# The discarded output of the norms' square activations: one 2-byte tile becomes two 1-byte tiles used by turns

## The chip, the cores and the metric

The kernel runs on one core of one Trainium2 chip. The metric is device time in microseconds: the median of several executions of the same program. Separately, one execution was recorded by the hardware profiler; everything said of single instructions comes from that one.

## What is computed

The input x has 128 batches of 128 rows by 512 columns (float32), and adj is a sparse 128 by 128 matrix. Two layers follow one another, each with a residual and a layer norm. The reference, cut to what matters:

```python
def _layernorm(x, eps=1e-5):
    m = mean(x, -1); v = var(x, -1)
    return (x - m) / sqrt(v + eps)

# layer 0: A = adj @ x[b]; W1 = W2 = adj, so C - A is the bias alone
out = max(relu(A[:, :, None, :] + (C - A)[:, :, :, None]), -1)   # = relu(rowmax(A) + b)
x = _layernorm(x + out)

# layer 1: 8 heads of 64
q, k, v = split(x @ w_qkv)
attn = softmax(where(adj == 0, -inf, q @ k.T * 64 ** -0.5))
o = (attn @ v) @ w_proj + b_proj
ln = (o - mean(o)) * rsqrt(var(o) + 1e-5) * gamma + beta
x = _layernorm(x + (o + ln))
```

So three variances are needed for each batch: one after layer 0, one inside layer 1 and one at its end.

## The kernel before

A batch is one tile of 128 partitions by 512 float32 columns, and four batches make a group; there are 32 groups. A batch passes through some sixty steps, each a small Python function that records one or a few instructions on one engine. A table of due times (`STEADY` for the groups in the middle, `FIRST` and `LAST` for those at the ends, lines 28 to 327) gives each step of each of the four batches its place relative to its group; `group_plan` collects all steps of all groups, the list is sorted by due time, and the instructions are recorded in that order. Every engine then works through its own queue strictly in this order. Semaphores are put in by the framework from the tiles that the instructions read and write: an instruction that writes a tile waits for those that read or wrote it before, on its own engine too.

Tiles that are reused have their buffer chosen by hand (`HOMES`, from line 342). In PSUM there are four single banks (`ps1`) and two double ones (`ps2`).

The steps that matter here, with their engines:

- TensorE: `dm` and `dd` form the dense products of the query, key and value projections. Each product is formed from three float32r products so that the accuracy of float32 is kept: `product` (lines 805 to 810) adds up eight matmuls in a bank called pm, `product_d` (812 to 815) four in a bank called pd. A name such as pd_(16, 5) means group 16, product 5.
- ScalarE: `main` (line 834) copies a pm bank into its place in qkT or v, which frees that bank; VectorE's `rest` (838) adds the pd bank. `exps` (894) takes the exponentials of the eight heads, each with an accumulated sum. `pln` (909) and `xpl` (708) split float32 tiles into two planes of 16 bits, which a DMA writes out and another reads back transposed. `norm0` (696) and `norm2` (1082) apply a norm.
- ScalarE again: `squares` (1038 to 1042) takes the sum of squares that a variance needs. It has three callers: `sq0` for layer 0 (two of the four batches of a steady group; the other two use VectorE's batch statistics, `bn`), `sq1` for the norm inside layer 1, and `sq2` for the last norm. The activation computes (sum - 512 x)^2, with the row sum as a bias pointer, and its accumulator gives the sum of the squares over a row in float32. This sum is all that is used.
- GpSimd: `sm`, `deviation` (1044 to 1049) and their like turn the sums into means and reciprocal deviations.

The squares themselves have to be written somewhere, though nobody reads them. They go to the tile `square`, 128 by 512 in bfloat16, allocated once at line 542. Each activation is shown in the profile as two rows: ACTIVATE, and ACTIVATION_READ_ACCUMULATOR, which delivers the sum.

In the last group the output projection is formed in plain float32 (`TWO["plain"]`, `po`, line 991) rather than from three products. The change leaves that as it is.

Of the kernel before, what the change touches and what calls it, by code (L numbers as in the profile page):

```python
# [13 lines left out]
AF = mybir.ActivationFunctionType  # L14
# [466 lines left out]
def tile_adj_resnorm_d2(  # L481
# [13 lines left out]
    B, T, D = x.shape  # L495
    P = 128
# [6 lines left out]
    scale = HD ** -0.5  # L503

    const = ctx.enter_context(tc.tile_pool(name="const", bufs=1))
# [33 lines left out]
    bias_sb = const.tile([P, D], FP, name="bias_sb")  # L539
    beta_sb = const.tile([P, D], FP, name="beta_sb")  # L540
    nc.vector.memset(mhalf, -0.5)
    square = const.tile([P, D], mybir.dt.bfloat16, name="square")
    nc.scalar.activation(mhalf, mhalf, AF.Copy)


# [102 lines left out]
    def sq0(b):  # L648
        mv, _, i = of_group(b)
        squares(xs[b], mv[:, i, :])  # L650
# [386 lines left out]

    def squares(src, s):

        nc.scalar.activation(  # L1040
            square, src, AF.Square, bias=s[:, 0:1], scale=-float(D), accum_out=s[:, 1:2],
        )

    def deviation(s, n):
# [6 lines left out]
    def sq1(b):  # L1051
        squares(os[b], s1s[b])
# [16 lines left out]
    def sq2(b):  # L1069
        squares(os[b], s2s[b])  # L1070
# [103 lines left out]
```

## Time and profile before

| | us |
|---|---|
| median of 3 executions | 1839.38 |
| lowest and highest of them | 1838.51 and 1841.58 |
| the profiled execution | 1842.82 |
| its span, first to last instruction | 1841.0 |

In the profiled execution ScalarE ran these groups of instructions among others:

| line | instruction | count | mean ns |
|---|---|---|---|
| 1040 | square of an o tile | 256 | 719 |
| 1040 | square of an xt tile | 62 | 722 |
| 1040 | reading the accumulator (o) | 256 | 190 |
| 644 | layer 0's addition, with a sum, 128 x 512 | 62 | 713 |
| 894 | exponential, 128 x 128 | 1016 | 392 |
| 909 | copy into planes, 128 x 2048 of 16 bits | 124 | 1891 |

How to read the profile: PE is TensorE's matmul row, PEld its weight loads, which run ahead of the matmuls they belong to; ACT is ScalarE, DVE VectorE, POOL GpSimd, SP the queue that issues DMAs. A row of a timeline gives the start, the duration, the engine, the source line, the operation and what it writes and reads; "x4" are four such in a row. Overlapping rows of one engine are two instructions in its pipeline. In a list of waits, "A <- B: total, times, longest" says that A stood idle until B was done. The chain is followed back from the last instruction, at each step to what released it.

### The profile page before, as it was taken

The page shows a single profiled execution, that of the slowest core. Times are in us where ns is not written, and L with a number is a line of the kernel's source. Part 1 is how long each engine was busy: PE and PEld are TensorE (multiplying, and loading weights), DVE is VectorE, ACT ScalarE, POOL GpSimd, SP SyncE. Part 2 cuts the span into 40 slices and gives each one's busy share as a digit, 9 for nine tenths or more (in the row PEclk, how much of TensorE's full clock was granted, in tenths as well). Part 3 has the DMA queues.
Part 4 walks back from the last instruction along what each step waited for, and adds up shares of the span by engine and source line. Part 5 has one row for each costly group of instructions (what it writes and reads, how often), then busy time and mean ns, then how long its engine had stood idle before and what let it go on. Part 6 is the DMA issues. An engine that isn't in the chain of part 4 may idle for free.

```text
span 1841.0 us, 32606 instructions
## 1 busy us (share of the span) xinstructions
PE 1808.0 (98%) x10525; PEld 1422.8 (77%) x10525; DVE 1527.8 (83%) x2539; ACT 1557.0 (85%) x3959; POOL 1287.5 (70%) x1932
## 2 busy tenths in 40 slices
PE   7999999999999999999999999999999999999996
PEld 4877787788777778787877877887877787878874
DVE  6988887888888888878888888888888888888875
ACT  5898888888888888988888988888988888879875
POOL 4265567767767767677676677677677676768878
PEclk9999999999999999999999999999999999999998
DMA  5566656567756576756576656676666776566552
GB/s 148 146 161 184 166 159 162 158 169 197 175 157 164 156 182 182 176 154 166 158 191 173 178 154 160 167 201 172 163 161 152 184 185 173 163 154 175 146 161 69
DMA packets 486714, 303.94 MB, mean 165 GB/s; under 512 B 399504, under 2 KB 403728, under 8 KB 486544
## 3 DMA queue, kind: packets, MB, share of 16 engines
q1 hardware_dynamic: 485680, 300.75, 62.2%
q8 instruction: 83, 1.36, 0.3%
q10 hardware_dynamic: 864, 1.12, 0.2%
q14 instruction: 87, 0.71, 0.1%
HBM read 73.20 MB, written 131.07 MB: 111 GB/s over the span
## 4 chain that ended last, share of the span: by engine, by line
PE 86%; POOL 5%; DVE 4%; ACT 2%; issue 2%; DMA 1%; SPq 0%; POOLq 0%; DVEq 0%; ACTq 0%
PE psc L855 6%; PE pav L941 6%; PE pa L624 5%; POOL sum L1046 1%; DVE o L1034 1%; POOL xb L1027 1%; POOL xb L1031 1%; DVE nmax L877 0%; DVE e L869 0%; POOL xb L1024 0%; DVE o L1061 0%; PE pv L769 0%; POOL sum L1045 0%; ACT e L894 0%; POOL od L741 0%
## 5 line engine op out<-in xcount | busy, mean ns | idle before, releaser
L894 ACT ACTIVATE e<-e,nmax 128x128 f32<-128x128 f32 x1016 | 392.6, 392 | 2.2 <-DVE nmax L877 2.1
L741 POOL TENSOR_TENSOR od<-oh,ol 128x512 fp32r<-128x512 f32 x124 | 164.6, 1328 | 139.4 <-DVE ol L959 77.5
L909 ACT COPY planes<-e 128x2048 uint16<-128x2048 uint16 x124 | 234.4, 1891 | 10.0 <-DVE e L903 5.1
L1046 POOL TENSOR_TENSOR sum<-sum,mhalf 128x1 f32<-128x1 f32 (+1 forms) x287 | 218.2, 760 | 23.9
L1040 ACT ACTIVATE square<-o,sum 128x512 bf16<-128x512 f32 x256 | 184.0, 719 | 22.7 <-DVE o L1034 14.4
L1031 POOL TENSOR_TENSOR xb<-xb,o 128x512 f32<-128x512 f32 x125 | 165.5, 1324 | 52.0 <-DVE o L1034 49.6
L894 ACT ACTIVATION_READ_ACCUMULATOR e<-e,nmax 128x1 f32 x1016 | 194.2, 191 | 0.0
L869 DVE SCALAR_TENSOR_TENSOR e<-psc,mask 128x1024 f32<-128x1024 f32 x127 | 152.5, 1220 | 43.9 <-PE psc L855 41.4
L1027 POOL TENSOR_TENSOR xb<-xb,beta_sb 128x512 f32<-128x512 f32 x128 | 165.7, 1294 | 2.9
L903 DVE TENSOR_TENSOR e<-e,sums 128x1024 f32<-128x1024 f32 x128 | 160.9, 1257 | 1.1
L1061 DVE SCALAR_TENSOR_TENSOR o<-o,sum,gamma_sb 128x512 f32<-128x512 f32 x128 | 103.9, 812 | 69.2 <-POOL sum L1049 65.7
L877 DVE TENSOR_REDUCE nmax<-e 128x8 f32<-128x1024 f32 x127 | 152.9, 1204 | 1.0
L735 POOL TENSOR_SCALAR oh<-oxh 128x512 fp32r<-128x512 f32 x31 | 64.8, 2090 | 116.8 <-DVE oxh L731 33.4
L708 ACT COPY xplanes<-xt 128x1024 uint16<-128x1024 uint16 x124 | 129.2, 1042 | 12.5 <-DMA rowsx<-xplanes 10.3
L624 PE MATMUL pa<-xt,adjT 128*128 128x512 f32 x256 | 133.9, 608 | 1.5 <-DVE rm L635 1.1
L855 PEld LDWEIGHTS psc<-qkT 64*128 64x128 f32 x2048 | 119.6, 188 | 19.8 <-issue 17.5
L855 PE MATMUL psc<-qkT 64*128 64x128 f32 x2048 | 132.4, 279 | 1.0 <-DVE o L1034 0.6
L941 PE MATMUL pav<-eT,v 128*64 128x128 f32 x2048 | 127.0, 276 | 0.9 <-ACT eT L932 0.8
L941 PEld LDWEIGHTS pav<-eT,v 128*64 128x64 f32 x2048 | 110.4, 137 | 17.9 <-issue 8.6
L1024 POOL TENSOR_SCALAR xb<-xb,sum 128x512 f32<-128x512 f32 x128 | 111.1, 868 | 12.2 <-DMA xb<-in_x_dram 12.1
L1034 DVE SCALAR_TENSOR_TENSOR o<-o,sum,xb 128x512 f32<-128x512 f32 x128 | 98.5, 769 | 24.0 <-POOL sum L1046 19.1
L696 ACT ACTIVATE xt<-xt,sum 128x512 f32<-128x512 f32 x128 | 103.3, 809 | 11.9 <-POOL sum L690 11.9
(4263 smaller groups left out, 5512.5 us busy)
## 6 DMA issues: line engine op xcount, KB each, us to landing
rows<-planes SPq DMA_DIRECT2D x124, 512.0 KB, 3.1
xt<-in_x_dram SPq DMA_DIRECT2D x128, 256.0 KB, 3.1
xb<-in_x_dram SPq DMA_DIRECT2D x128, 256.0 KB, 2.9
out_dram<-o SPq DMA_DIRECT2D x128, 256.0 KB, 3.2
rowsx<-xplanes SPq DMA_DIRECT2D x124, 256.0 KB, 2.5
wraw<-in_L_gnn_w_qkv_dram SPq DMA_DIRECT2D x8, 256.0 KB, 3.5
xT<-rowsx SPq DMA_TRANSPOSE x124, 3.8
eT<-rows SPq DMA_TRANSPOSE x124, 5.1
```

The lines of the kernel that those rows point to most:

```text
L624: nc.tensor.matmul(pa[b], adjT, xs[b], start=True, stop=True)
L741: engine.tensor_tensor(d, h.bitcast(FP), l.bitcast(FP), op=ALU.subtract)
L855: nc.tensor.matmul(psc[:, s, hp, :], qkT[hs, hp, i, :], qkT[hs, KC + hp, i, :], start=not with_mask, stop=not with_mask or hp == HP - 1,)
L877: nc.vector.tensor_reduce(nmaxs[b], es[b], AX.X, ALU.max, negate=True)
L894: nc.scalar.activation(es[b][:, j, :], src[:, j, :], AF.Exp, bias=nmax[:, j : j + 1], scale=by, accum_out=sums[b][:, j : j + 1],)
L903: nc.vector.tensor_tensor(es[b], es[b], sums.pop(b)[:, :, None].to_broadcast([P, H, P]), op=ALU.mult,)
L909: nc.scalar.copy(pl, es.pop(b).rearrange("p h m -> p (h m)").bitcast(U16).rearrange("p (m s) -> p s m", s=2),)
L941: nc.tensor.matmul(pavs[b][s * HD : (s + 1) * HD, hp, :], v[:, h * HD : (h + 1) * HD], eT[:, s * HP + hp, :], start=True, stop=True,)
L1027: nc.gpsimd.tensor_tensor(xbs[b], xbs[b], beta_sb, op=ALU.add)
L1031: engine.tensor_tensor(xbs[b], xbs[b], os[b], op=ALU.add)
L1040: nc.scalar.activation(square, src, AF.Square, bias=s[:, 0:1], scale=-float(D), accum_out=s[:, 1:2],)
L1046: nc.gpsimd.tensor_tensor(s, s, mhalf[:, :n], op=ALU.pow)
```

## The change

The tile of 512 bfloat16 values a partition becomes a tile of two halves, each of 512 one-byte unsigned integers a partition. A counter flips at every call of `squares`, and the activation writes to the half that it names. The accumulated sum, its operands and all else stay as they are. The whole of it:

```diff
@@ -539,7 +539,8 @@
     nc.vector.memset(mhalf, -0.5)
-    square = const.tile([P, D], mybir.dt.bfloat16, name="square")
+    junk = const.tile([P, 2, D], mybir.dt.uint8, name="squares")
+    turn = [0]
     nc.scalar.activation(mhalf, mhalf, AF.Copy)
@@ -1037,8 +1038,9 @@
     def squares(src, s):
 
+        turn[0] ^= 1
         nc.scalar.activation(
-            square, src, AF.Square, bias=s[:, 0:1], scale=-float(D), accum_out=s[:, 1:2],
+            junk[:, turn[0], :], src, AF.Square, bias=s[:, 0:1], scale=-float(D), accum_out=s[:, 1:2],
         )
```

## The prediction

> **What bounds the kernel now.** I read the page first (busy shares, then the chain), then the weight-load queue's list of waits, then the timelines of one group, and last each semaphore record of the trace against the wait values in the program.
>
> ```profile
> PE 1808.0 (98%) x10525; PEld 1422.8 (77%) x10525; DVE 1527.8 (83%) x2539; ACT 1557.0 (85%) x3959; POOL 1287.5 (70%) x1932
> ...
> PE 86%; POOL 5%; DVE 4%; ACT 2%; issue 2%; DMA 1%; SPq 0%; POOLq 0%; DVEq 0%; ACTq 0%
> ...
> L1040 ACT ACTIVATE square<-o,sum 128x512 bf16<-128x512 f32 x256 | 184.0, 719 | 22.7 <-DVE o L1034 14.4
> ```
>
> TensorE is busy all the time and carries the chain; ScalarE holds 2% of it. So what the squares cost ScalarE matters only where TensorE waits for ScalarE. The page shows no such wait, since matmul ends are modelled; the weight loads do. In the list of waits of the weight-load queue from 276 to 1600 us, this line stands once for every group from 5 to 28, 24 times, at 0.4 or 0.5 us:
>
> ```profile
> PEld pd_(16, 5)_10122 L815 <- ACT qkT L834: 0.5, 1, 0.5
> PEld pd_(17, 5)_10745 L815 <- ACT qkT L834: 0.5, 1, 0.5
> ```
>
> Group 16 on the PE timeline (start, us, what):
>
> ```profile
> 921.24 0.39 PE L809 MATMUL pm_(16, 6)_10101<-x_h,w_h 128*128 128x512 f32 x1
> 921.47 0.39 PE L810 MATMUL pm_(16, 6)_10101<-x_l,w_l 128*128 128x512 f32 x1
> ...
> 921.92 0.39 PE L810 MATMUL pm_(16, 6)_10101<-x_l,w_l 128*128 128x512 f32 x1
> 922.34 1.19 PE L815 MATMUL pd_(16, 5)_10122<-x_d,w_d 128*128 128x512 f32 x4
> 923.37 0.39 PE L809 MATMUL pm_(16, 5)_10134<-x_h,w_h 128*128 128x512 f32 x1
> ```
>
> Matmuls start 0.227 us apart (921.24 to 921.92 is three steps). From 921.92 to 923.37 are five steps, 1.135 us unhindered; they took 1.45. TensorE loses about 0.31 us here, in each of the 24 groups. It waits for a PSUM bank that ScalarE empties with the copy into qkT. ScalarE ahead of that copy:
>
> ```profile
> 914.29 0.71 ACT L1040 ACTIVATE square<-o,sum 128x512 bf16<-128x512 f32 x1
> 914.90 0.19 ACT L1040 ACTIVATION_READ_ACCUMULATOR square<-o,sum 128x1 f32 x1
> 915.13 0.72 ACT L1040 ACTIVATE square<-o,sum 128x512 bf16<-128x512 f32 x1
> 915.76 0.18 ACT L1040 ACTIVATION_READ_ACCUMULATOR square<-o,sum 128x1 f32 x1
> 915.98 0.72 ACT L1040 ACTIVATE square<-xt,sum 128x512 bf16<-128x512 f32 x1
> 916.61 0.19 ACT L1040 ACTIVATION_READ_ACCUMULATOR square<-xt,sum 128x1 f32 x1
> 916.70 1.89 ACT L909 COPY planes<-e 128x2048 uint16<-128x2048 uint16 x1
> ...
> 921.71 0.57 ACT L834 ACTIVATE qkT<-pm_(16, 8)_10087 128x512 f32<-128x512 f32 x1
> ```
>
> See the seams. 914.90 + 0.19 = 915.09, and the next square starts at 915.13: 0.04 after. At 916.61 + 0.19 = 916.80 the copy had already started (916.70): 0.10 before. A square that follows a square lacks the overlap that every other pair has. From 907.87 (a qkT copy that waits for TensorE) to the end of the copy at 921.71 ScalarE never idles for another engine: this run of work, started by TensorE and awaited by it, is 0.31 us too long.
>
> **What the Trainium skill says.** "ScalarE: Activation LUTs", section What ACT_TABLE_LOAD costs, has one element a cycle for fp32 and bf16 alike, 280 ns + 0.833 ns an element with a pointer bias, and back-to-back activations overlapping by about 93 ns. That gives 706 ns for 512; the squares took 705 to 753, and the seams overlap by 0.09 to 0.10 us: agreed. Of one-byte outputs no page states a rate, and nothing in the trace writes one. "Perfetto Trace Analysis", section DVE / Act Engine Instruction, has the reported end at the acknowledged write, from which the semaphore goes out; so a wait for one's own predecessor costs the whole overlap and a little more, as the 0.04 shows. The same page, Identifying the Most-Contended Engine, calls matmul busy time a poor measure and weight loads a better one: so it is here. Under Identifying Dependency Chains it says that further waits go into a separate instruction ahead; the trace has 78 such on line 1040.
>
> **The change part by part.**
> *Instructions.* Both programs have the same instructions in the same order on every engine, but for 22 more wait-only ones on ScalarE. The tile takes 1024 bytes a partition as before (512 x 2, now 2 x 512 x 1), at the same address. No DMA and no queue moves.
>
> *Removed: the wait for the square just before.* All squares write one tile, so each waits for the last. In 88 places two squares stand side by side; in 84 of them this wait, and nothing else, ended last in the trace (23 or 24 ns before the start); the other four, in the last 13 us, wait for VectorE. With two halves by turns a square waits for the last but one, done long before (the third, at 915.98, would ask for the one that ended at 915.09). Each such place gains 0.04 + 0.09 = 0.13 us.
>
> *Where it counts.* A steady group has three places: 915.13 and 915.98 in the run ahead of TensorE's wait, and 934.10, after which ScalarE waits 0.39 us for a DMA at 936.01 anyway (gain nothing). So the qkT copy comes 0.26 us sooner. Nothing else holds it: in the semaphore records the next-latest release of what lies between came 0.5 us or more before its start (planes 506 ns, o 7.7 us, xt 1.4 us, qkT 1.2 us). 0.26 is less than the 0.31 lost, so all of it reaches TensorE: 24 x 0.26 = 6.2 us.
>
> *What is late next.* The following bank, pm_(16, 5), is freed by the qkT copy at 922.35, which follows TensorE's own pm_(16, 6) and doesn't move: released 0.42 us before its use, about 0.15 us of it spare at the weight load, and a weight load can be 0.1 us late unnoticed (one at 926.06 was 0.17 late and cost 0.06). Enough, or short by 0.02. Other waits later in the group (VectorE's qkT additions) follow TensorE and move with it.
>
> *Two more places.* pd_(2, 9) at 141.18 and pm_(29, 6) at 1650.42 wait for a qkT copy behind one such pair: 0.13 each, 0.26.
>
> *Added.* About 27 xplanes copies get a second wait, for ScalarE itself, long fulfilled. Squares with two waits start 83 ns after VectorE's release, those with one 24, so this may cost 0.06 us each. It falls at 936.01, followed by 0.13 us of idle time at 939.00 and almost 3 us at 952.57: nothing. Without that cover, 1.5 us. Ten squares lose a second wait; at the end four of these lie 0.06 us nearer to VectorE, but GpSimd sets the pace there: nothing.
>
> *One-byte outputs.* From below: no gain, since fp32 and two-byte outputs already run at one rate. From above: if a one-byte write ran at half rate, 512 x 0.833 = 0.43 us a square. I take nothing, by the equal rates of the other types.
>
> *Sum.* 6.2 + 0.26 = 6.5 us. The profiled execution took 1842.82 (span 1841.0), so 1836.3 there; it lay 3.4 above the median. From the median 1839.38: 1832.9.
>
> **The rivals.**
> *A: given back.* Another chain through VectorE or GpSimd is almost as long, and TensorE gets half: 24 x 0.13 = 3.1, 1836.3. For it: the pm_(16, 5) release leaves little, and TensorE waits again at pd_(16, 11). Against: that wait is a round trip with TensorE itself, and the other waits in the group have 0.1 us or more.
> *B: the seam isn't the wait.* If squares miss the overlap for another cause, nothing changes: 1839.4. Against: squares after any copy overlap by 0.10 us, and exponentials with the same bias pointer and accumulator, side by side, overlap too (904.83 + 0.19, next 904.92).
> *C: slower, by the one-byte write.* Between 907.87 and 921.71 stand four squares (908.36 and the three shown). The gain of 0.26 is used up at 0.065 us more a square. Beyond that TensorE waits longer: at 0.21 a square 24 x (0.85 - 0.26) = 14 us, 1854; at the full 0.43, 24 x 1.45 = 35, 1874. For it: this output type is in no row. Against: time follows elements, not bytes, in every row of ScalarE (the uint16 copy of 2048 elements takes 1891 ns, 0.833 each and a constant).
>
> **How the numbers follow.** Likeliest 0.72 (1831 to 1835.5), A 0.14, B 0.05, C 0.09. Forecast 1832.9. A measurement of this kernel can tell about 0.2%, 3.7 us, from no change; the three runs shown spread over 3.1. Faster by more: 0.72 and a fifth of A, 0.75. Within: the rest of A and B, 0.16. Slower: C, 0.09. The range 1830.5 to 1837.0 holds the likeliest case and most of A, and leaves out B, C and the likeliest one's ends. Its upper end takes in the 1.5 us of the uncovered waits.
>
> **What would show it.** Squares at about 720 ns on a uint8 tile; seams between squares at -0.09 in place of +0.04; the 24 lines of pd_(g, 5) in the weight-load waits gone or under 0.2 us; five steps of 1.2 us in place of 1.45 there; groups nearer by 0.26 us. It is wrong if squares last over 780 ns, if the seams stay, or if the lines go and other weight loads wait as long.

## The result, and the profile after

| | before, us | after, us |
|---|---|---|
| median of 5 executions each, same chip | 1839.80 | 1833.06 |
| lowest and highest | 1838.51 and 1841.58 | 1832.4 and 1834.64 |
| the profiled execution | 1842.82 | 1834.2 |
| its span | 1841.0 | 1832.4 |

The ratio is 0.9963, with a 95% interval of 0.9949 to 0.9978: 6.7 us faster. The two profiled executions lie 8.6 us apart. Part of that is not the change: the first qkT copy of all, which runs before the first square, started at 27.77 us instead of 29.47. These 1.7 us are a difference of the two starts.

Three lines of the page after: the busy shares, the chain by engine, and the group of the squares (busy us, mean ns, idle time ahead of them).

```profile
PE 1802.5 (98%) x10525; PEld 1420.9 (78%) x10525; DVE 1526.9 (83%) x2539; ACT 1549.0 (85%) x3959; POOL 1288.8 (70%) x1932
...
PE 86%; POOL 6%; DVE 3%; ACT 2%; issue 1%; DMA 1%; SPq 0%; POOLq 0%; ACTq 0%; DVEq 0%
...
L1042 ACT ACTIVATE squares<-o,sum 128x512 uint8<-128x512 f32 x256 | 183.2, 717 | 21.5 <-DVE o L1035 15.2
```

The page hardly tells the two kernels apart: TensorE bounds both, and one square lasts 717 ns instead of 719. The difference is in how squares follow each other. ScalarE in group 16, from the three squares in a row to the qkT copy that TensorE awaits and the one after it (start, us, what):

```profile
908.37 0.73 ACT L1042 ACTIVATE squares<-o,sum 128x512 uint8<-128x512 f32 x1
908.99 0.20 ACT L1042 ACTIVATION_READ_ACCUMULATOR squares<-o,sum 128x1 f32 x1
909.08 0.73 ACT L1042 ACTIVATE squares<-o,sum 128x512 uint8<-128x512 f32 x1
909.69 0.20 ACT L1042 ACTIVATION_READ_ACCUMULATOR squares<-o,sum 128x1 f32 x1
909.79 0.73 ACT L1042 ACTIVATE squares<-xt,sum 128x512 uint8<-128x512 f32 x1
...
915.52 0.58 ACT L835 ACTIVATE qkT<-pm_(16, 8)_10087 128x512 f32<-128x512 f32 x1
916.43 0.60 ACT L835 ACTIVATE qkT<-pm_(16, 6)_10101 128x512 f32<-128x512 f32 x1 [0.33 <-PE pm_(16, 6)_10101 L811]
```

908.99 + 0.20 is 909.19, and the next square had started at 909.08: it overlaps its predecessor by 0.11 us. At the second seam (909.69 + 0.20, then 909.79) it is 0.10. Before, both seams had a gap of 0.04.

The list of the weight loads' waits from 276 to 1600 us. Of the 24 lines for pd_(g, 5) four are left:

```profile
PEld pd_(5, 5)_3269 L816 <- ACT qkT L835: 0.5, 1, 0.5
PEld pd_(10, 5)_6384 L816 <- ACT qkT L835: 0.4, 1, 0.4
PEld pd_(20, 5)_12614 L816 <- ACT qkT L835: 0.4, 1, 0.4
PEld pd_(15, 5)_9499 L816 <- ACT qkT L835: 0.4, 1, 0.4
```

And TensorE at the same place in group 16:

```profile
916.00 0.39 PE L811 MATMUL pm_(16, 6)_10101<-x_l,w_l 128*128 128x512 f32 x1
916.24 1.11 PE L816 MATMUL pd_(16, 5)_10122<-x_d,w_d 128*128 128x512 f32 x4
917.18 0.40 PE L810 MATMUL pm_(16, 5)_10134<-x_h,w_h 128*128 128x512 f32 x1
```

The five steps from the last matmul of pm_(16, 6) to the first of pm_(16, 5) take 917.18 - 916.00 = 1.18 us, where they took 1.45. Steps of 0.227 would give 1.135. From one pm_(g, 6) to the next an undisturbed group took 55.75 us before and takes 55.49 now: 0.26 less. From the pm_(g, 6) of group 5 to that of group 28, which are 23 such periods, the time went from 1284.11 to 1278.31 us: 5.8 less.

The same place can be read in all 24 groups of both traces. Beyond 1.135 us the five steps cost 7.67 us in sum before. After, they cost 1.93: 0.02 to 0.05 us in each of twenty groups, 0.22 to 0.32 in each of the four with a line above. The one step after them, beyond 0.227 us, cost 0.07 us in sum before and 0.34 after. So TensorE gained 5.5 us here (7.67 + 0.07 - 1.93 - 0.34).

**The four groups that are left.** ScalarE in group 10, with the idle time ahead of an instruction and its releaser in brackets:

```profile
575.84 0.71 ACT L1042 ACTIVATE squares<-xt,sum 128x512 uint8<-128x512 f32 x1
576.45 0.19 ACT L1042 ACTIVATION_READ_ACCUMULATOR squares<-xt,sum 128x1 f32 x1
577.26 1.90 ACT L910 COPY planes<-e 128x2048 uint16<-128x2048 uint16 x1 [0.61 <-DVE e L904]
```

The seam is mended here too, but the copy behind it waits 0.61 us for VectorE, which scales the attention weights at line 904. In groups 5 and 20 the copy waits for the same line, 0.52 and 0.48 us. In group 15 the wait is 0.10 us and too short for a row to name its releaser, but it is VectorE there too:

```profile
853.69 1.31 DVE L904 TENSOR_TENSOR e<-e,sums 128x1024 f32<-128x1024 f32 x1
...
855.03 1.90 ACT L910 COPY planes<-e 128x2048 uint16<-128x2048 uint16 x1
```

853.69 + 1.31 is 855.00, and the copy starts 0.03 us later, as it does in the other three. In group 16 VectorE's release came 506 ns ahead of this copy before the change and 215 ns ahead after it.

The change did not make VectorE late. In the kernel before, the same copy waits for it in groups 5, 15, 20 and 25, by 0.34, 0.34, 0.12 and 0.14 us. Two of these:

```profile
302.43 1.90 ACT L909 COPY planes<-e 128x2048 uint16<-128x2048 uint16 x1 [0.34 <-DVE e L903]
...
860.93 1.90 ACT L909 COPY planes<-e 128x2048 uint16<-128x2048 uint16 x1 [0.34 <-DVE e L903]
```

Where VectorE ends last, a mended seam ahead of it gains nothing. What makes VectorE late was followed in group 10 of the kernel after alone. There VectorE stands idle for 1.05 us up to 570.65, until GpSimd's sums (L1048) are done, and is not idle again before line 904 ends. In group 16 the same idle time is 0.10 us. The sums come behind a small GpSimd instruction (L1051) of 0.67 us that takes 0.22 in group 16. The kernel before has slow small GpSimd instructions in the same groups too (0.65 us in group 10, 0.68 in group 15). What slows them in about every fifth group was not tried.

### The profile page after: what moved, and what is told of

Read it like the earlier page. It is cut to its first block, busy times and chain, and to the rows that moved or that the text cites. A ratio compares the mean times of both kernels' runs of the same rounds, so it can differ in the third digit from the quotient of the medians.

```text
span 1832.4 us, 32628 instructions
## 1 busy us (share of the span) xinstructions
PE 1802.5 (98%) x10525; PEld 1420.9 (78%) x10525; DVE 1526.9 (83%) x2539; ACT 1549.0 (85%) x3959; POOL 1288.8 (70%) x1932
## 4 chain that ended last, share of the span: by engine, by line
PE 86%; POOL 6%; DVE 3%; ACT 2%; issue 1%; DMA 1%; SPq 0%; POOLq 0%; ACTq 0%; DVEq 0%
PE psc L856 7%; PE pav L942 6%; PE pa L625 5%; POOL xb L1028 1%; POOL sum L1048 1%; POOL xb L1032 1%; ACT e L895 1%; DVE o L1035 1%; POOL x_d L742 1%; POOL od L742 1%; POOL xb L1025 1%; POOL sum L1051 0%; DVE o L1063 0%; POOL sum L1047 0%; PE pv L770 0%
## 5 line engine op out<-in xcount | busy, mean ns | idle before, releaser
L1048 POOL TENSOR_TENSOR sum<-sum,mhalf 128x1 f32<-128x1 f32 (+1 forms) x287 | 217.3, 757 | 23.9
L1042 ACT ACTIVATE squares<-o,sum 128x512 uint8<-128x512 f32 x256 | 183.2, 717 | 21.5 <-DVE o L1035 15.2
L1025 POOL TENSOR_SCALAR xb<-xb,sum 128x512 f32<-128x512 f32 x128 | 115.6, 904 | 9.3 <-DMA xb<-in_x_dram 9.2
```

The lines of the kernel that those rows point to most:

```text
L1042: nc.scalar.activation(junk[:, turn[0], :], src, AF.Square, bias=s[:, 0:1], scale=-float(D), accum_out=s[:, 1:2],)
L1048: nc.gpsimd.tensor_tensor(s, s, mhalf[:, :n], op=ALU.pow)
```

## The experiments

My theory: the wait of a square for its predecessor on the one discarded tile kept the two from overlapping; in a steady group only the two seams ahead of the qkT copy of product 8 count, and TensorE gains what that copy gains. The rivals: the shorter output type makes the gain (or costs something); any time taken from ScalarE helps, wherever it lies; or the gain stops at another wait. All runs were timed against the kernel before on the same chip, in five rounds except the last two, in three.

### Is it one byte, or the turns?

`one_byte_one_tile`: the kernel before with the type changed alone.

```diff
-    square = const.tile([P, D], mybir.dt.bfloat16, name="square")
+    square = const.tile([P, D], mybir.dt.uint8, name="square")
```

> One tile of 512 one-byte values for all squares, without turns: each square waits for the one before it again. If the wait between neighbouring squares is what was removed, nothing is gained: 1839.8 us, ratio 1.000, the 24 weight-load waits of pd_(g, 5) back at 0.4 to 0.5 us each. If the one-byte output is what helps (fewer bytes written), all or most of the 6.7 us stay: 1833. If one-byte writes were slower, over 1841.

Measured 1839.21 against 1839.64: 0.9995 [0.9987, 1.0004], no difference. The view by tile of this run (lowest, median and highest ns) and its timeline:

```profile
L1040 ACT ACTIVATE square<-o,sum x256: 706/721/754, 103.9 to 1830.6; 128x512 uint8<-128x512 f32 x128
```

```profile
910.83 0.72 ACT L1040 ACTIVATE square<-o,sum 128x512 uint8<-128x512 f32 x1
911.44 0.20 ACT L1040 ACTIVATION_READ_ACCUMULATOR square<-o,sum 128x1 f32 x1
911.68 0.72 ACT L1040 ACTIVATE square<-o,sum 128x512 uint8<-128x512 f32 x1
```

A one-byte output takes 721 ns, as the two-byte one did. The gap is there: 911.44 + 0.20 = 911.64, next start 911.68. All 24 lines of pd_(g, 5) stay. So the type neither pays nor costs; the gain is that of the turns. The type matters in another way: two halves of one byte fit in the 1024 bytes that one two-byte tile took. Two halves of two bytes don't fit in the memory that is left, so turns with the two-byte type weren't run; that the type has no part in it rests on this run.

### Do only the seams ahead of the awaited copy count?

Two versions of the changed kernel without the counter. The squares all write half 0, but those of the norm inside layer 1 write half 1 for one of the four batches, which mends some seams and leaves others.

```diff
-    turn = [0]
...
-    def squares(src, s):
-
-        turn[0] ^= 1
+    def squares(src, s, half=0):
+
...
-            junk[:, turn[0], :], src, AF.Square, ...
+            junk[:, half, :], src, AF.Square, ...
...
-        squares(os[b], s1s[b])
+        squares(os[b], s1s[b], int(b % G == 0))    # two_seams_ahead
+        squares(os[b], s1s[b], int(b % G == 2))    # one_seam_elsewhere
```

> The second half is used by one square in a group alone, the sq1 of batch 0, so that the two seams ahead of TensorE's wait open and the third (between the sq1 of batches 3 and 2) stays. By my theory that is all the steady gain: 24 x 0.26 = 6.2 us, 1833.6. If the gain follows the ScalarE time that is saved, wherever it is saved, two thirds of 6.7: 1835.3. If one byte is what helps: 1833 as with any other use of the halves.

> The second half is used by the sq1 of batch 2 alone, so that only the third seam opens, after which ScalarE waits for a DMA anyway. By my theory no gain: 1839.8, at most 0.5 us from groups at the ends. If the gain follows the ScalarE time saved, a third of 6.7: 1837.6. If one byte is what helps: 1833.

`two_seams_ahead` took 1834.13 against 1839.64, 0.9969 [0.9958, 0.9981]; lines of pd_(g, 5) are left in groups 5, 10, 15 and 25. That is the change's gain within what the intervals tell apart. `one_seam_elsewhere`, which mends the third seam (the one before a wait for a DMA), took 1840.53, 1.0005 [0.9997, 1.0013]: nothing. Its list of weight-load waits still has this line for each of the 24 groups:

```profile
PEld pd_(16, 5)_10122 L815 <- ACT qkT L834: 0.5, 1, 0.5
```

So it is the place of the seams that pays, not their number. The rival that any time taken from ScalarE helps falls by the second run: a third of the gain would be 1837.6. The first alone would not decide it, since two thirds of the gain, 1835.3, lie within its interval.

### Is it the time of the qkT copy?

`before_copy_sooner` has the kernel before with its one tile and all its seams; only the due time of one copy is changed, so that it goes one instruction sooner, ahead of a `norm0`. If TensorE just waits for that copy, this must bring the same gain. `after_copy_sooner` makes the same move in the changed kernel.

```diff
-        'main': [..., -25.069, -12.689, ...],
+        'main': [..., -25.069, -13.500, ...],
```

> The kernel before with its squares unchanged; the due time of the ScalarE copy of product 8 is moved by 0.8 us, so that it stands one instruction sooner in ScalarE's order, ahead of a norm of 0.71 us. By my theory TensorE's wait of 0.31 us goes whole in 24 groups: 7.4 us, 1832.4, and the pd_(g, 5) lines leave the weight-load waits, though all seams stay at +0.04. If the squares' seams cost time in any other way, or the period is bound elsewhere, 1839.8.

> The changed kernel with the copy of product 8 one instruction sooner as well. Both edits shorten the same stretch of ScalarE work ahead of the same wait of TensorE, so by my theory the gains don't add: the sooner copy alone came to a period of 55.51 us, the turns alone to 55.49, since TensorE's next bank, pm_(g, 5), waits for the copy of its own product 6. What is left are the four groups (5, 10, 15, 20) in which the wait of about 0.3 us is still there after the change: 1.2 us at most, 1832.0 to 1833.1. If the two were separate gains: 1827.5.

`before_copy_sooner`: 1834.27 against 1839.64, 0.9972 [0.9964, 0.9979]; `after_copy_sooner`: 1833.45 against 1840.26, 0.9967 [0.9955, 0.998]. No line of pd_(g, 5) is left in either from 276 to 1600 us. The gains don't add: the same wait is removed once. The second lies a little above the 1832.0 to 1833.1 expected, by less than its interval can tell. An undisturbed group takes nearly the same in both, 55.51 and 55.49 us.

The first brought 5.4 us where a complete removal of the stall at pd_(g, 5), 24 x 0.31, would have been 7.4. ScalarE and then TensorE in its group 17:

```profile
970.80 1.05 ACT L708 COPY xplanes<-xt 128x1024 uint16<-128x1024 uint16 x1
971.75 0.59 ACT L834 ACTIVATE qkT<-pm_(17, 8)_10710 128x512 f32<-128x512 f32 x1
972.24 0.81 ACT L696 ACTIVATE xt<-xt,sum 128x512 f32<-128x512 f32 x1
973.10 0.60 ACT L834 ACTIVATE qkT<-pm_(17, 6)_10724 128x512 f32<-128x512 f32 x1
```

```profile
972.67 0.39 PE L810 MATMUL pm_(17, 6)_10724<-x_l,w_l 128*128 128x512 f32 x1
972.90 1.07 PE L815 MATMUL pd_(17, 5)_10745<-x_d,w_d 128*128 128x512 f32 x4
973.80 0.44 PE L809 MATMUL pm_(17, 5)_10757<-x_h,w_h 128*128 128x512 f32 x1
974.08 0.39 PE L810 MATMUL pm_(17, 5)_10757<-x_l,w_l 128*128 128x512 f32 x1
```

From 972.67 to 973.80 the five steps take 1.13 us: no stall at pd_(17, 5) any more. But the next step, 973.80 to 974.08, takes 0.28 instead of 0.227. The bank of pm_(17, 5) is freed by the copy that starts at 973.10, and this copy can't start before TensorE has finished pm_(17, 6) itself. That is the next limit, a round trip of TensorE with ScalarE, and it doesn't move when ScalarE gets faster ahead of it: in `after_copy_sooner`, with the seams mended as well, this step still takes 0.28. The period fell by 0.24 of the 0.31. Times 24 that is 5.8 us, near the 5.4 measured.

### Put the time back

If 0.26 us less ahead of the copy gives the gain, about as much more ahead of it must take it away, and the same extra elsewhere must cost nothing. My first pair missed.

```diff
+    spare = const.tile([P, 128], mybir.dt.uint8, name="spare")
+    nc.vector.memset(spare, 0)
...
     def xpl(b):
+        if b % G == 0:               # extra_ahead; == 3 in extra_elsewhere
+            nc.scalar.copy(spare, spare)
```

> The changed kernel with one useless ScalarE copy of 128 one-byte values, in every group, just ahead of the xplanes copy of batch 0, so within the stretch that TensorE waits for. From the rows of ScalarE it should add about 0.2 us[...]. By my theory the stretch has nothing to spare: 24 to 30 times 0.2 us, 1838 to 1839. If total ScalarE time or its idle time absorbed it: 1833.

> The same useless copy, as often, ahead of the xplanes copy of batch 3, where ScalarE waits for a DMA anyway. By my theory it costs nothing: 1833 (up to 0.5 more from the ends). If ScalarE time counts wherever it lies: 1838, as with the copy ahead.

1857.56 and 1857.01 against 1840.26, 1.0095 [1.0081, 1.0109] and 1.0093 [1.0079, 1.0107]: both far slower, wherever the copy stood. So this was not ScalarE. In both traces TensorE's float32r matmuls lie further apart, and a group took 56.35 us. The new tile had pushed all later ones 128 bytes along. Two runs below test this. For the question itself I took the extra work from memory that was there, four unused columns beside the constant -0.5, and made it an activation with two pointers:

```diff
-    mhalf = const.tile([P, 8], FP, name="mhalf")[:, :G]
+    mh = const.tile([P, 8], FP, name="mhalf")
+    mhalf, spare = mh[:, :G], mh[:, G:]
...
-    nc.vector.memset(mhalf, -0.5)
+    nc.vector.memset(mh, -0.5)
...
     def norm2(b):
+        if b % G == 2:               # extra_ahead_same_layout; == 0 in extra_elsewhere_same_layout
+            nc.scalar.activation(spare, spare, AF.Identity, bias=mhalf[:, 0:1], scale=mhalf[:, 1:2])
```

> The two runs before moved all later tiles by 128 bytes with their new tile, and every float32r matmul took longer, so they tell nothing of ScalarE. Here a useless ScalarE operation (four values, two pointers, about 0.38 us, less 0.10 of overlap) works on unused columns of an existing tile, so that no address moves. It stands ahead of the norm2 of batch 2 in every group, within the stretch that TensorE waits for. By my theory: 24 to 30 times 0.28, less at most 1 us of slack in all: 1839 to 1841. If ScalarE has slack there: 1833.

> The same operation, as often, ahead of the norm2 of batch 0, after which ScalarE waits for a DMA. By my theory it costs nothing: 1832.5 to 1834. If ScalarE time counts wherever it lies: as with the other, 1839 to 1841.

ScalarE in the first, ahead of the awaited copy, and the list of its weight-load waits for two groups:

```profile
914.64 1.90 ACT L911 COPY planes<-e 128x2048 uint16<-128x2048 uint16 x1
916.43 0.40 ACT L1085 ACTIVATE mhalf<-mhalf 128x4 f32<-128x4 f32 x1
916.72 0.82 ACT L1087 ACTIVATE o<-o,sum 128x512 f32<-128x512 f32 x1
```

```profile
PEld pd_(10, 5)_6392 L817 <- ACT qkT L836: 0.7, 1, 0.7
...
PEld pd_(16, 5)_10136 L817 <- ACT qkT L836: 0.5, 1, 0.5
```

The useless activation costs ScalarE 916.72 - 916.43 = 0.29 us. The kernel took 1840.68 against 1839.83, 1.0009 [1.0002, 1.0015]: the whole gain is gone. All 24 lines are back, and the period is 55.77 us, 0.28 more than 55.49. In the second the same activation stands where ScalarE would soon have waited:

```profile
930.89 0.38 ACT L1085 ACTIVATE mhalf<-mhalf 128x4 f32<-128x4 f32 x1
931.17 0.80 ACT L1087 ACTIVATE o<-o,sum 128x512 f32<-128x512 f32 x1
931.97 1.04 ACT L710 COPY xplanes<-xt 128x1024 uint16<-128x1024 uint16 x1
...
935.21 0.63 ACT L739 ACTIVATE oh<-oxh 128x512 fp32r<-128x512 f32 x1 [0.39 <-DVE oxh L733]
```

In the changed kernel without the extra work the xplanes copy was the one that waited for a DMA, 0.18 us in this group:

```profile
929.47 1.05 ACT L709 COPY xplanes<-xt 128x1024 uint16<-128x1024 uint16 x1 [0.18 <-DMA rowsx<-xplanes]
```

With it the copy starts at once, at 931.17 + 0.80 = 931.97: the extra work has filled that wait, and behind it ScalarE still waits 0.39 us for VectorE. The DMA's wait isn't there in every group. In the kernel before, it and the wait for VectorE two instructions later come to 0.27 us or more together in each of the 23 groups from 276 to 1600 us, now the one and now the other.

The run took 1833.58, 0.9965 [0.9952, 0.9978], with four lines left (groups 10, 14, 20, 25) and a period of 55.49 us: the gain of the change, with 0.28 us more work a group on ScalarE. The same work, in two places, costs 7 us or nothing.

### What the first pair had measured

The changed kernel with an unused tile after the halves, and nothing else: 128 bytes, then 64.

```diff
+    pad = const.tile([P, 128], mybir.dt.uint8, name="pad")    # 64 in pad_64
+    nc.vector.memset(pad, 0)
```

> The changed kernel with an unused tile of 128 bytes behind the two halves, written once at the start. Nothing else than the addresses of the later tiles changes. If they made the two runs slower, 1856 to 1858 and float32r matmuls 230 to 237 ns apart in place of 227; if the useless copies did, 1833.

> The same with 64 bytes. I have no theory of the rule; if any shift of the moving operands against the weights costs the same, 1857; if only a part of an address counts, anything from 1833 to 1857, and faster than 1833 if the present place isn't the best.

1855.62 and 1854.36 against 1839.83: 1.0088 [1.0072, 1.0103] and 1.0079 [1.0066, 1.0093]. TensorE in the run with 128 bytes, one product, then in the run with 64:

```profile
924.10 0.40 PE L812 MATMUL pm_(16, 8)_10089<-x_h,w_h 128*128 128x512 f32 x1
924.34 0.39 PE L813 MATMUL pm_(16, 8)_10089<-x_l,w_l 128*128 128x512 f32 x1
924.57 0.40 PE L812 MATMUL pm_(16, 8)_10089<-x_h,w_h 128*128 128x512 f32 x1
924.80 0.39 PE L813 MATMUL pm_(16, 8)_10089<-x_l,w_l 128*128 128x512 f32 x1
```

```profile
920.99 1.10 PE L818 MATMUL pd_(16, 7)_10063<-x_d,w_d 128*128 128x512 f32 x4
921.92 1.10 PE L818 MATMUL pd_(16, 4)_10070<-x_d,w_d 128*128 128x512 f32 x4
```

Steps of 0.24 and 0.23 us in the first; four in 921.92 - 920.99 = 0.93, or 0.2325 each, in the second. In the kernels without a pad the step is 0.227. The clock granted to TensorE from 276 to 1600 us is 1.00 of full speed in both, as in the changed kernel, so it isn't the clock. So the layout alone costs what the first pair had lost; the copy added to it was not needed.

## Why the prediction was right

Predicted 1832.9, measured 1833.06: a gain of 6.5 us against 6.7. The mechanism is the one predicted. That the number came so near is in part luck: the main term was too high by 0.7 us, gains elsewhere that no run attributes made up for it, and the interval of the ratio leaves the gain open by 2.7 us either way. By its steps:

- *The gap is a wait for the own predecessor.* Shown. With turns the seams overlap by 0.10 to 0.11 us; with the same type on one tile they keep the gap of 0.04. Rival B falls. The 0.13 us a seam is what was found. One reading was too wide: it isn't so that "every other pair" overlaps. In the kernel before, the xplanes copy at 920.04 starts 0.03 us after the norm at 919.21 has ended (919.21 + 0.80 = 920.01), since it reads what that norm writes. That pair loses its overlap to a wait that is needed, much as the squares did to one that is not.
- *Only two seams of a steady group count.* Shown by the two runs that mend some seams alone, and by the extra work in two places. The wait for a DMA behind the third was read in one group; in others it is a wait for VectorE that makes the third seam free.
- *0.26 us, 24 times: 6.2.* Too high: 5.5 measured at this place. The 0.26 is right for an undisturbed group, where the period fell from 55.75 to 55.49. The count is not: in four groups the wait is still there, since the copy into planes starts late, for VectorE in all four. The prediction's "next-latest release", planes at 506 ns, was read in one group and held for all. The trace that it was read from shows no such reserve in groups 5, 15, 20 and 25, where the copy already waits for VectorE. Twenty groups would have given 5.2. Both executions also have single longer periods: before, by 0.95 us into group 15, 0.27 into group 20 and 0.55 into group 25; after, by 0.5 into group 10, 0.3 into group 11, and 0.4 and 0.2 into groups 20 and 21. They blur the 5.8 of the 23 periods; the 5.5 is read at the place itself.
- *Two more places, 0.13 each.* The profiled executions gained 0.95 us between groups 1 and 2 and 0.58 from group 28 to 29, and lost 0.8 in the tail. One execution of each can't say how much of it is the change; the sum of the term, 0.26, is below what was measured there.
- *What is late next: pm_(g, 5), "enough, or short by 0.02".* The right bank, a little too mild. In the changed kernel the step into it is mostly 0.24, at times 0.27, instead of 0.227, and with the copy moved sooner 0.28 or 0.29. It costs up to 0.04 us in the changed kernel and about 0.06 with the copy moved, the more, the less is lost at pd_(g, 5). It is the reason why no more than about 0.25 of the 0.31 is to be had from ScalarE here. Rival A (half of it given back) overrated it.
- *The added second waits: nothing.* The mended seam alone costs nothing where it stands ahead of the DMA wait, and the changed kernel loses nothing against `two_seams_ahead` beyond the intervals. A cost of 1.5 us for them isn't seen; it wasn't measured by itself.
- *One-byte outputs: nothing.* Shown: medians of 714 and 723 ns for the squares of o and of xt after, 721 and 722 before, and the ratio 0.9995 of the type alone. Rival C needed 0.065 us a square. The argument from the equal rates of other types, on which the Trainium skill ("ScalarE: Activation LUTs", section What ACT_TABLE_LOAD costs) and this trace agreed, carried over to a type that neither had shown.
- *From the profiled execution to the median.* The sum was taken off the profiled execution and then off the median. The medians differ by 6.7, the profiled executions by 8.6; the start alone, ahead of any square, accounts for 1.7 of the second number. Taking the difference, and not the profiled time itself, was what made the forecast hold.

The busy shares did not show the stall, those of the weight loads (77% before, 78% after) as little as those of the matmuls (98% and 98%); the list of what the weight loads waited for did. No version measured is faster than the changed kernel by more than the intervals: `after_copy_sooner` lies 0.0004 of the ratio behind it.

## What to carry to other kernels

Write results that nobody reads to two tiles by turns. The framework makes an instruction wait for the last writer of its output even where the values don't matter, and on ScalarE that wait cost 0.13 us each time that the writer was the instruction just before, by losing the overlap with it. What such a saving is worth is decided by place: find the wait of the bounding engine that ends last, go back over the stretch of work that leads to it, and count only the seams in that stretch. Before counting on the whole of it, look for the next release that doesn't move with the first, and read its reserve in every group, not in one: here the trace from before the change had four groups without any.

## What the hardware showed that I had not expected

*The address of tiles changes the rate of TensorE's float32r matmuls.* An unused tile of 128 or 64 bytes a partition made the kernel 0.88% and 0.79% slower than the one before, so about 1.2% slower than the changed kernel without it. It moved the tiles allocated after it. The parts of x that go into the float32r matmuls lay at addresses of 192 modulo 512 bytes in both kernels, at 320 with 128 bytes more and at 256 with 64 more; the tiles of w_qkv and w_proj stayed at 192. The spacing of the float32r matmuls with 512 columns went from 0.227 us to 0.229 to 0.237. That holds for those that stream x past the weights, and also for those of v and of the output projection, which stream the unmoved weights past tiles that moved. So it isn't the address of the streamed operand alone. Plain float32 matmuls kept theirs (0.429 us in layer 0, in all three). A tile 512 bytes smaller, in `one_byte_one_tile`, leaves the address modulo 512 as it was and changed nothing. Which relation of addresses makes the difference is open; these are three layouts. Someone who adds a small tile to such a kernel, in an experiment above all, should compare the spacing of the matmuls before anything else.

*A disturbance in about every fifth group.* VectorE is late for the copy into planes in groups 5, 10, 15 and 20 of the changed kernel and in groups 5, 15, 20 and 25 of the kernel before, and two other versions keep TensorE's wait in four groups as well (5, 10, 15, 25 in one; 10, 14, 20, 25 in the other). In group 10 it stood behind a GpSimd instruction that took 0.67 us instead of 0.22. What slows that instruction stays open.
